# A four-layer graph network on one core: transposes moved from TensorE to DVE blocks and transfers, and three engines' order written out

## The chip, the cores and the metric

One Trainium2 chip, one of its cores. The metric is the device time of one execution in microseconds (us); the program runs on core 0 alone, in float32 throughout. The engines are called by their short names: PE (TensorE, matmuls), PEld (its weight loads), DVE (VectorE), ACT (ScalarE), POOL (GpSimd) and SP (SyncE, here only a queue that issues DMAs).

## The reference

128 graphs of 64 nodes with 256 features pass through four layers, each followed by a residual sum and a layer norm. Every layer uses the same weighted adjacency `adj` (128 x 64 x 64), which is not symmetric.

```python
# --- layer 0: five node groups (25 of the 64 nodes), two graph convolutions each
x = _layernorm(x + _L0_gnn_ref(x, adj, W1, b1, W2, b2, fusion_w))
# --- layer 1
A = adj + eye;  dinv = A.sum(-1) ** -0.5
x = _layernorm(x + (dinv[:, :, None] * A * dinv[:, None, :]) @ (x @ W) + b)
# --- layer 2
An = adj / (adj.sum(2, keepdims=True) + 1e-9);  c = h = x @ W.T
out = w[0] * c
for k in (1, 2, 3):
    c = An @ c;  out = out + w[k] * c
x = _layernorm(x + leaky_relu(out + b, 0.2))
# --- layer 3: five steps of a gated recurrent cell, A = (adj != 0)
h = x
for l in range(5):
    agg = A.T @ (h @ weight[l])
    r = sigmoid(agg @ Wir + h @ Whr + b);  z = sigmoid(agg @ Wiz + h @ Whz + b)
    n = tanh(agg @ Win + bin + r * (h @ Whn + bhn))
    h = (1 - z) * n + z * h
x = _layernorm(x + h * mask)
```

## The kernel before

**Tiling.** The 128 graphs are cut into 16 chunks of 8 graphs. Two graphs lie side by side on the 128 partitions (64 nodes each), and a chunk holds four such pairs of graphs: a tile of node states is 128 x 4 x 256. An adjacency of two graphs is a 128 x 128 block-diagonal square. Layer 3 keeps its state the other way round, features on the partitions (`hT`, `hn`: 128 x 2 x 512), so that the gate products stream 256 columns; products 1 to 7 of each gate are a scheme with seven products (factored weights `V`, `WHH`; differences `Ta`, `Th` from `sums`, L746, on POOL) in place of eight.

**Stages.** The first 300 us are layer 0 over all graphs, in 16 units; layers 1 and 2 of chunks 0 and 1 are fitted into its last units (`early`, two instances of `mid`). Then come the folded weights, and then the loop, which is layer 3 for all chunks. Chunks run in pairs: step s works on chunk `rows[s % 2]`, so the two chunks of a pair take turns, five layers each, ten steps to a pair. Steps of a pair are called 0 to 9 here; step 8 is layer 5 of the even chunk, step 9 that of the odd one. While a pair is in the loop, `mid` (L220) does layers 1 and 2 of the next pair in parts, each part ending at a `yield`; `next(filler)` in `step` runs one part. In a step, PE multiplies for x; the other chunk w is finished at the start (`new(3)`), and gets its messages near the end.

**`mid`.** Part 1, on DVE: the block-diagonal `Ab` is the loaded adjacency times a 0/1 `pair` mask (L227), then `A01`, row sums, `dg`, `An`. Part 2: four PE transposes of `Ab` (L259), evicted by DVE into `poly` (L262) and `AT1` (L264, L265). Part 3: a product `pp`, its eviction (L273) and layer 1's gather (L212). Part 4: `xt` plus bias (L277) and the last polynomial. Parts 5 and 6: layer 1's products, norm. Parts 7 to 9: layer 2 and its norm.

**The change of pairs.** After its fifth layer a chunk's `hn` is turned back into node order: `flip` (L881) turns 32 x 32 blocks on DVE (L888), writes them to DRAM (L893) and reads them back permuted (four reads, L897) into `h`. `output` (L991) adds `h` to `xt` with eight DVE instructions (L998) and takes the norm's statistics; `close` (L1001) scales on ACT and stores. The new chunk's first `hT` comes from layer 2's result by eight PE transposes (L810) and two ACT copies (L817), in `state_of_layer2` (L813).

**What sets the order.** PE's order is written out by hand for the whole program (`manual_schedule`), ACT's for the loop. DVE, POOL and the DMA queue SP are ordered by a planner with costs and due times of its own; each engine then runs its list in order and waits at semaphores. `issue_after` and `high_priority` are hints to that planner. A tile with `bufs=n` has n buffers that take turns; a new use waits for the last reader of the old one. PSUM is two pools of 5 (`pg`) and 3 (`pt`) banks.

Of the kernel before, what the change touches and what calls it, by code (L numbers as in the profile page):

```python
# [24 lines left out]
CB = 8  # L25
# [43 lines left out]
def gnn_stack(  # L69
# [21 lines left out]
    c_pair: bass.AP,  # L91
# [34 lines left out]
    def norm_stats(y, by="v", n=NP, r=128):  # L126

        by = (by * n)[:n]
        st = small.tile([128, NP, 6], F32, name="st")
        mv = small.tile([128, NP, 2], F32, name="mv")  # L130
        for p in range(n):
            nc.vector.bn_stats(st[:r, p, :], y[:r, p, :])  # L132
            nc.vector.bn_aggr(mv[:r, p, :], st[:r, p, :])
        ve = small.tile([128, NP], F32, name="ve")
        nc.vector.tensor_scalar(ve[:r, :n], mv[:r, :n, 1], EPS_LN, None, op0=ALU.add)  # L135
        rs = small.tile([128, NP], F32, name="rs")
        nc.gpsimd.tensor_tensor(rs[:r, :n], ve[:r, :n], mhalf[:r, :n], ALU.pow)  # L137
        nb = None
        if "a" in by:
            nb = small.tile([128, NP], F32, name="nb")  # L140
            nc.vector.scalar_tensor_tensor(nb[:r, :n], mv[:r, :n, 0], -1.0, rs[:r, :n], op0=ALU.mult, op1=ALU.mult)
        return mv, rs, nb
# [11 lines left out]
    def layernorm(y, by="v", n=NP, r=128):  # L154
        norm_apply(y, *norm_stats(y, by, n, r), by, n, r)
# [10 lines left out]
    av = adj.rearrange("(c p two) n m -> c (two n) p m", p=NP, two=2)  # L166
# [20 lines left out]
    def load_adj(c):  # L187
        a64 = keep.tile([128, NP, N], F32, name="a64", bufs=2)
        nc.sync.dma_start(a64, av[c])
        adjs[c] = a64  # L190
# [27 lines left out]
    state = {}  # L218

    def mid(c, first=False):  # L220

        a64 = adjs.pop(c)


        Ab = keep.tile([128, NP, 128], F32, name="Ab", bufs=1)
        with tc.issue_after(evictions[-1].ins):
            nc.vector.tensor_mul(  # L227
                Ab.rearrange("p q (b m) -> p q b m", b=2),
                a64[:, :, None, :].to_broadcast([128, NP, 2, N]),
                pair[:, None, :, :].to_broadcast([128, NP, 2, N]),  # L230
            )
        A01 = keep.tile([128, NP, 128], F32, name="A01", bufs=4)
        nc.vector.tensor_scalar(A01, Ab, 0.0, None, op0=ALU.not_equal)
        rsum = small.tile([128, NP], F32, name="rsum")
        with tc.issue_after(evictions[-1].ins):
            nc.vector.tensor_reduce(rsum, a64, AX.X, ALU.add)
# [5 lines left out]
        dinv1 = inv_sqrt(rdeg, NP, 128, "d1")  # L242
# [13 lines left out]
        AT1 = keep.tile([128, NP, 128], F32, name="AT1", bufs=1)  # L256
        p = psum("pT1").rearrange("p (q n) -> p q n", q=NP)
        for q in range(NP):
            nc.tensor.transpose(p[:, q, :], Ab[:, q, :], ident)  # L259

        with tc.high_priority():
            nc.vector.scalar_tensor_tensor(poly, p, cw[:, 3:4], poly, op0=ALU.mult, op1=ALU.add)  # L262

        nc.vector.tensor_add(AT1, p, ident[:, None, :].to_broadcast([128, NP, 128]))  # L264
        nc.vector.tensor_mul(AT1, AT1, dinv1[:, :, None].to_broadcast([128, NP, 128]))  # L265
# [34 lines left out]
        norm_apply(xt, *norm)  # L300
# [21 lines left out]
        norm_apply(xt, *norm)  # L322
# [14 lines left out]
    with ExitStack() as c0:  # L337
# [101 lines left out]
        def hidden(i):  # L439
            u = UNITS[i]  # L440
            ag0 = AG.pop(i)
            hg = keep.tile([128, 4, 512], F32, tag="NI", name="hg", bufs=2)
            for e in range(4):
                p = psum0("ph")[:, : u.cols]
                for k in range(2):
                    nc.tensor.matmul(  # L446
                        p, W1[:, u.g, k, e * 128 : (e + 1) * 128], ag0[:, k, : u.cols], start=k == 0, stop=k == 1
                    )
                relus.append(
                    nc.scalar.activation(hg[:, e, : u.cols], p, AF.Relu, bias=b1[:, u.g * 4 + e : u.g * 4 + e + 1])  # L450
                )
            HG[i] = hg
# [97 lines left out]
        zero = keep.tile([128, 4, 512], F32, tag="NI", name="zero", bufs=2)[:, 0, :]  # L550
# [50 lines left out]
        for i in range(-2, NU + 1):  # L601
# [60 lines left out]
            elif i == 1:  # L662
                with tc.issue_after(powers[-1].ins):
                    pair = const_later(c_pair, [128, 2, N], "pair")
# [29 lines left out]
            elif i == g0:  # L694
                for c in (0, 1):
                    load_adj(c)
            elif i == g0 + 1:
                for c in (0, 1):
                    load_x(c)
        for _ in early:  # L700
            pass
# [98 lines left out]
    class Chunk:  # L800
# [19 lines left out]

        def messages(self):
            src = halves(self.xt)
            if self.l:
                h = self.h
                src = lambda q, k: h[:, q, 2 * k : 2 * k + 2, :]
            self.agg = gather(src, self.A01, "agg", work, "agg", 2)
            self.ta = sums(self.agg, "a")
# [20 lines left out]
        def n(self, i):  # L848
            if i == 1:
                self.NI = keep.tile([128, 2, 2, NP * 128], F32, tag="NI", name="NI", bufs=2)  # L850
                self.gn = Gates(
                    self.NI, [[(V[self.l], 2, self.agg, self.ta)], [(WHH, 2, self.hT, self.th)]], "n"
                )
            self.gn.product(i)

        def new(self, i):
# [3 lines left out]
            if i == 2:  # L860
                self.hn = work.tile([128, 2, NP * 128], F32, tag="hT", name="hn", bufs=3)
# [19 lines left out]
        def flip(self, half):  # L881
# [3 lines left out]
            if not half:  # L885
                self.h = work.tile([128, NP, NP, 64], F32, name="h", bufs=1)
            t = work.tile([128, NP, 2, 2, 32], F32, name="flip", bufs=2)
# [103 lines left out]
        def output(self):  # L991
# [7 lines left out]
            self.norm = norm_stats(self.xt, "a")  # L999
# [31 lines left out]
    before = ended = None  # L1031
    filler = iter(())

    def step(s):
        nonlocal before, ended, filler
        x, w = rows[s % 2], before
        nxt = None
        x.rz(1)
        if w:
            w.new(3)  # L1040
        x.rz(2)
        x.rz(5)
        next(filler, None)
# [4 lines left out]
        next(filler, None)  # L1048
        x.rz(7)
        x.new(2)  # L1050
        x.n(6)
        x.sigmoid(7)
        if w and w.l == L - 1 and w.c + 2 < NCH:
            nxt = Chunk(w.c + 2)
            nxt.state_of_layer2(1)
        x.n(5)
        if nxt:
            nxt.state_of_layer2(0)
# [4 lines left out]
        if ended:  # L1063
            ended.close()
            ended = None
# [4 lines left out]
        elif w:  # L1070
            w.output()
            ended = w
            if nxt:
                nxt.messages()
                rows[(s + 1) % 2] = nxt
        x.sigmoid(3)
# [6 lines left out]
    for s in range(NCH * L - 1):  # L1083
        u, t = s // (2 * L) * 2, s % (2 * L)
        if t == 0:
            for _ in filler:
                pass
            if u + 2 < NCH:
                for c in (u + 2, u + 3):
                    load_adj(c)  # L1090
                    load_x(c)
                filler = both(mid(u + 2), mid(u + 3))
        with tc.manual_schedule(engines={mybir.EngineType.Activation}):
# [10 lines left out]
    x.NI = keep.tile([128, 2, 2, NP * 128], F32, tag="NI", name="NI", bufs=2)  # L1104
# [5 lines left out]
    norm = norm_stats(w.xt)  # L1110
# [10 lines left out]
def _constants():  # L1121
    ident = np.eye(128, dtype=np.float32)
    b128 = np.arange(128) // N
    pair = np.repeat((b128[:, None] == np.arange(2)[None]).astype(np.float32), N, axis=1).reshape(128, 2, N)
# [11 lines left out]
    return {"ident": ident, "pair": pair, "block0": block, "eye0": eye}  # L1136
# [44 lines left out]
```

## Time and profile before

| what | number |
|---|---|
| median of 3 runs | 2156.74 us (2156.57 to 2156.82) |
| the profiled execution, its own time | 2156.53 us |
| its span, first to last instruction | 2154.8 us, 31383 instructions |
| granted PE clock, mean | 0.999 |
| DMA | 133.05 MB, 386411 packets, mean 62 GB/s |
| a pair's ten steps | 231.1 us (windows from 564.6 on) |

In what follows, a line of a group reads: line of the kernel, engine, operation, output <- input (buffer numbers left out), shapes and count | busy us in total, mean ns of one | idle time of the engine just before, and what ended it. PSUM tiles named `pT1`, `pT3`, `pT4` all appear as `pT`. A line of the timeline reads: start in us, length in us, engine, line, operation, count of merged ones, and in brackets how long the engine had been idle and who released it. A matmul's length includes the pipeline, so the pitch of matmuls is read from starts. A float32 matmul call appears as two instructions, a transpose as one.

### The profile page before, as it was taken

How to read it: one execution, taken by the hardware profiler on the slowest of the kernel's cores; microseconds unless marked ns; L12 is line 12 of the kernel's file. 1: busy time of each engine (PE TensorE's matmuls, PEld its weight loads, DVE VectorE, ACT ScalarE, POOL GpSimd, SP SyncE). 2: the span in 40 equal slices, each digit the busy share in tenths (PEclk: the TensorE clock that was granted, in tenths of full speed). 3: DMA queues.
4: the chain of work that ended last, by engine and by line, in shares of the span. 5: the costliest groups of instructions: out<-in, count | busy, mean ns of one | idle time of the engine just before them, and what ended most of it. 6: DMA issues, size and time to landing. Idle time of an engine off the chain costs nothing.

```text
span 2154.8 us, 31383 instructions
## 1 busy us (share of the span) xinstructions
PE 2112.3 (98%) x10914; PEld 1844.1 (86%) x10914; DVE 1558.6 (72%) x3821; ACT 991.4 (46%) x2034; POOL 592.8 (28%) x634
## 2 busy tenths in 40 slices
PE   9999999999999999999999999999999999999997
PEld 6777888988888888988888889888898889888886
DVE  3345667776878778867887697868877787768666
ACT  3343344444454444444545445444445454454444
POOL 3311131322322323322322232223322232322222
PEclk9999999999999999999999999999999999999999
DMA  6632110221221222121321222122221221122121
GB/s 168 180 126 63 54 38 23 51 51 46 68 69 40 55 52 74 48 54 48 85 50 40 59 62 62 40 59 62 66 53 40 56 73 40 48 51 72 47 59 40
DMA packets 386411, 133.05 MB, mean 62 GB/s; under 512 B 353102, under 2 KB 381260, under 8 KB 386252
## 3 DMA queue, kind: packets, MB, share of 16 engines
q1 hardware_dynamic: 381380, 125.79, 22.6%
q0 software_dynamic: 2160, 4.83, 0.9%
q8 instruction: 87, 1.43, 0.3%
q10 hardware_dynamic: 2712, 0.42, 0.1%
q14 instruction: 72, 0.59, 0.1%
HBM read 73.30 MB, written 57.67 MB: 61 GB/s over the span
## 4 chain that ended last, share of the span: by engine, by line
PE 84%; DVE 13%; DMA 1%; issue 1%; POOL 1%; ACT 0%; SPq 0%; ACTq 0%; DVEq 0%; POOLq 0%
PE parz L769 22%; PE pdrz L769 11%; PE pan L769 11%; PE pa L212 8%; PE pbrz L769 5%; PE pdn L769 5%; PE ps L462 5%; PE ph L446 4%; PE pbn L769 3%; PE pd L311 3%; DVE xt L998 2%; PE pd L290 2%; PE pa L430 1%; DVE st L132 1%; PE po L484 1%
## 5 line engine op out<-in xcount | busy, mean ns | idle before, releaser
L786 ACT COPY c<-parz 128x512 f32<-128x512 f32 x240 | 140.1, 584 | 407.6 <-PE parz L769 407.6
L769 PE MATMUL parz<-Th,WHH 128*128 128x256 f32 x960 | 286.6, 380 | 11.5 <-ACT c L786 11.5
L769 PE MATMUL parz<-Ta,V 128*128 128x256 f32 x960 | 285.5, 379 | 0.0
L910 ACT ACTIVATE NI<-NI,bih 128x256 f32<-128x256 f32 x316 | 159.4, 507 | 186.7 <-DVE NI L905 183.7
L844 ACT ACTIVATE RZ<-RZ,brz 128x256 f32<-128x256 f32 x474 | 215.0, 503 | 51.2 <-DVE RZ L788 41.9
L749 POOL TENSOR_TENSOR Ta<-agg 128x512 f32<-128x512 f32 x80 | 102.3, 1279 | 490.6 <-ACT agg L214 490.1
L769 PEld LDWEIGHTS parz<-Th,WHH 128*128 128x128 f32 x960 | 177.8, 190 | 35.6 <-ACT c L786 13.9
L769 PEld LDWEIGHTS parz<-Ta,V 128*128 128x128 f32 x960 | 182.4, 190 | 24.8
L137 POOL TENSOR_TENSOR rs<-ve,mhalf 128x4 f32<-128x4 f32 (+2 forms) x65 | 68.2, 1049 | 484.7 <-DVE ve L135 432.7
L214 ACT COPY agg<-pa 128x512 f32<-128x512 f32 x160 | 93.0, 586 | 151.4 <-PE pa L212 151.4
L792 DVE TENSOR_TENSOR NI<-pbn,c 128x512 f32<-128x512 f32 x79 | 54.3, 688 | 139.0 <-ACT c L786 139.0
L749 POOL TENSOR_TENSOR Th<-hn 128x512 f32<-128x512 f32 x64 | 81.5, 1274 | 244.3 <-DVE hn L913 244.3
L904 DVE SCALAR_TENSOR_TENSOR NI<-NI,bhh,RZ 128x256 f32<-128x256 f32 x237 | 142.0, 599 | 4.9
L769 PE MATMUL pan<-Ta,V 128*128 128x256 f32 x474 | 141.4, 380 | 0.8 <-ACT c L786 0.7
L769 PE MATMUL pan<-Th,WHH 128*128 128x256 f32 x474 | 141.0, 379 | 0.0
L786 ACT COPY c<-pan 128x512 f32<-128x512 f32 x237 | 137.2, 579 | 7.8 <-PE pan L769 4.4
L912 DVE TENSOR_TENSOR RZ<-RZ 128x256 f32<-128x256 f32 x316 | 128.7, 407 | 1.9
L212 PEld LDWEIGHTS pa<-A,h 128*128 128x128 f32 x1024 | 124.4, 192 | 4.3 <-issue 1.0
L913 DVE TENSOR_TENSOR hn<-RZ,NI 128x256 f32<-128x256 f32 x316 | 125.7, 415 | 3.2
L788 DVE TENSOR_TENSOR NI<-pdn,c 128x512 f32<-128x512 f32 x79 | 54.4, 689 | 99.3 <-ACT c L786 99.3
L212 PE MATMUL pa<-A,h 128*128 128x128 f32 x1024 | 124.8, 275 | 0.6 <-issue 0.6
L888 DVE STREAM_TRANSPOSE flip<-hn 128x512 f32<-128x512 f32 x156 | 108.9, 698 | 0.0
(229 smaller groups left out, 4887.6 us busy)
## 6 DMA issues: line engine op xcount, KB each, us to landing
hb<-flip SPq DMA_DIRECT2D x156, 256.0 KB
h<-hb SPq DMA_DIRECT2D x624, 64.0 KB
out_dram<-xt SPq DMA_DIRECT2D x30, 256.0 KB
W<-in_w_dram SPq DMA_DIRECT2D x10, 512.0 KB
xt<-xb SPq DMA_DIRECT2D x32, 156.0 KB
xo<-in_x_dram SPq DMA_DIRECT2D x9, 512.0 KB
xb<-xo SPq DMA_DIRECT2D x9, 512.0 KB
xt<-xa SPq DMA_DIRECT2D x32, 100.0 KB
```

The costliest lines, as they stand in the source:

```text
L212: nc.tensor.matmul(p[:, q * 128 : (q + 1) * 128], src(q, k), m[:, q, :], start=True, stop=True)
L214: nc.scalar.copy(a[:, k, :], p)
L462: nc.tensor.matmul(p[: u.rows[t], t - v, :], hg[:, e, u.off[t] : u.off[t] + u.rows[t]], W2[:, u.g, e, :], start=e == 0, stop=e == 3,)
L749: nc.gpsimd.tensor_sub(t[:, 0:2, :], a[:, :, H:], a[:, 0, :].rearrange("p (s n) -> p s n", s=2))
L769: nc.tensor.matmul(bank[:, g, :], w[:, q, i - 1, :], rhs, start=i in (1, 2, 5) and g == 0 and m == 0, stop=m == len(side) - 1, skip_group_ ...
L786: nc.scalar.copy(c, self.a)
L844: nc.scalar.activation(v, self.g.a[:, q, :] if i == 4 else v, AF.Sigmoid, bias=brz[:, 2 * q + j : 2 * q + j + 1])
L888: nc.vector.transpose(t.rearrange("p r q j f -> p q j r f"), self.hn[:, :, half * H : (half + 1) * H].rearrange("p j (q r f) -> p q j r f" ...
L904: nc.vector.scalar_tensor_tensor(n[:, j, f], h, bhh[:, 4 + j : 5 + j], r[:, j, f], op0=ALU.add, op1=ALU.mult)
L910: nc.scalar.activation(n, n, AF.Tanh, bias=bih[:, 4 + j : 5 + j])
L912: e.tensor_mul(d, d, z)
L913: e.tensor_add(self.hn[:, j, f], d, n)
```

## The change

- Layer 2's result is turned into `hT` by `state_by_transfer`: a DVE block transpose of each half, one write to DRAM and four reads per half. It is called a step earlier than the PE version was, at layer 5 of x. The first two chunks keep `state_of_layer2`. `sums` of the new `hT` is called at the next step's start.
- The adjacency comes in twice: into the diagonal blocks of `Ab`, which is now one buffer zeroed once, and in 32 x 32 blocks into `aB`, which DVE turns into the diagonal blocks of `AT1`, zeroed once too. The mask product, the constant `pair` and the PE transposes in `mid` are gone. Loads of adjacency and states are placed at steps 3 and 8.
- The filler runs at two places of a step, at one in step 0. `norm_stats` is split: the pow and `nb` are in `norm_root`. `output`'s norm is finished a step later, and `close` is a step later and at the step's start. New messages come before `output`.
- ACT, SP and POOL all follow the program's order over the whole loop.
- Buffers: `NI` one instead of two, with `hn` of the last layer written into it; `h` two instead of one; `hg` of layer 0 takes turns between two pools.

```diff
-    def norm_stats(y, by="v", n=NP, r=128):
+    def norm_stats(y, n=NP, r=128):
...
+        return mv, ve
+
+    def norm_root(mv, ve, by="v", n=NP, r=128):
+        by = (by * n)[:n]
         rs = small.tile([128, NP], F32, name="rs")
         nc.gpsimd.tensor_tensor(rs[:r, :n], ve[:r, :n], mhalf[:r, :n], ALU.pow)
...
     def load_adj(c):
-        a64 = keep.tile([128, NP, N], F32, name="a64", bufs=2)
-        nc.sync.dma_start(a64, av[c])
-        adjs[c] = a64
+        aB = keep.tile([128, NP, N], F32, name="aB", bufs=1)
+        ac = adj[c * CB : (c + 1) * CB].rearrange("(p two) n m -> two n p m", two=2)
+        for two in range(2):
+            b = slice(two * N, (two + 1) * N)
+            nc.sync.dma_start(Ab[b, :, b], ac[two])
+        for two in range(2):
+            for r in range(2):
+                o = two * N + 32 * r
+                for v in range(2):
+                    nc.sync.dma_start(
+                        aB[o : o + 32, :, 32 * v : 32 * v + 32], ac[two, 32 * v : 32 * v + 32, :, 32 * r : 32 * r + 32]
+                    )
+        adjs[c] = aB
...
+    Ab = keep.tile([128, NP, 128], F32, name="Ab")
+    AT1 = keep.tile([128, NP, 128], F32, name="AT1")
     def mid(c, first=False):
...
         with tc.issue_after(evictions[-1].ins):
-            nc.vector.tensor_mul(
-                Ab.rearrange("p q (b m) -> p q b m", b=2),
-                a64[:, :, None, :].to_broadcast([128, NP, 2, N]),
-                pair[:, None, :, :].to_broadcast([128, NP, 2, N]),
-            )
-        A01 = keep.tile([128, NP, 128], F32, name="A01", bufs=4)
+            for two in range(2):
+                b = slice(two * N, (two + 1) * N)
+                nc.vector.transpose(AT1[b, :, b], aB[b])
...
-            nc.vector.tensor_reduce(rsum, a64, AX.X, ALU.add)
+            nc.vector.tensor_reduce(rsum, Ab, AX.X, ALU.add)
...
-        p = psum("pT1").rearrange("p (q n) -> p q n", q=NP)
-        for q in range(NP):
-            nc.tensor.transpose(p[:, q, :], Ab[:, q, :], ident)
-
+        dinv1 = inv_sqrt(rdeg, NP, 128, "d1")
         with tc.high_priority():
-            nc.vector.scalar_tensor_tensor(poly, p, cw[:, 3:4], poly, op0=ALU.mult, op1=ALU.add)
-
-        nc.vector.tensor_add(AT1, p, ident[:, None, :].to_broadcast([128, NP, 128]))
-        nc.vector.tensor_mul(AT1, AT1, dinv1[:, :, None].to_broadcast([128, NP, 128]))
+            nc.vector.scalar_tensor_tensor(poly, AT1, cw[:, 3:4], poly, op0=ALU.mult, op1=ALU.add)
+
+        nc.vector.tensor_add(AT1, AT1, ident[:, None, :].to_broadcast([128, NP, 128]))
+        for two in range(2):
+            b = slice(two * N, (two + 1) * N)
+            nc.vector.tensor_mul(AT1[b, :, b], AT1[b, :, b], dinv1[b, :, None].to_broadcast([N, NP, N]))
...
+                    for t in (Ab, AT1):
+                        nc.gpsimd.memset(t, 0.0)
...
+        def state_by_transfer(self):
+            self.hT = work.tile([128, 2, NP * 128], F32, tag="hT", name="hT", bufs=3)
+            for j in range(2):
+                t = work.tile([128, NP, NP, 32], F32, tag="flip2", name="flip2", bufs=2)
+                nc.vector.transpose(
+                    t.rearrange("p a q n -> p q a n"),
+                    self.xt[:, :, j * 128 : (j + 1) * 128].rearrange("p q (a i) -> p q a i", a=NP),
+                )
+                hb = dram.tile([NP, NP, NP, 32, 32], F32, name="hb2", bufs=2)
+                nc.sync.dma_start(
+                    hb.rearrange("a q r i n -> (r i) (a q) n"), t.rearrange("p a q n -> p (a q) n")
+                )
+                for a in range(NP):
+                    nc.sync.dma_start(
+                        self.hT[32 * a : 32 * (a + 1), j, :].rearrange("p (g n) -> p g n", n=32),
+                        hb[a].rearrange("q r i n -> i (q r) n"),
+                    )
...
     def step(s):
-        nxt = None
+        nxt = coming.pop() if coming else None
         x.rz(1)
         if w:
             w.new(3)
+        if closing:
+            closing.close()
+        closing, ended = ended, None
+        if nxt:
+            nxt.th = sums(nxt.hT, "h")
         x.rz(2)
         x.rz(5)
-        next(filler, None)
+        if s % (2 * L):
+            next(filler, None)
...
-        next(filler, None)
         x.rz(7)
         x.new(2)
+        c = s // (2 * L) * 2 + {3: 3, 8: 4}.get(s % (2 * L), NCH)
+        if c < NCH:
+            load_adj(c)
+            load_x(c)
         x.n(6)
         x.sigmoid(7)
-        if w and w.l == L - 1 and w.c + 2 < NCH:
-            nxt = Chunk(w.c + 2)
-            nxt.state_of_layer2(1)
+        if closing:
+            closing.norm = norm_root(*closing.norm, "a")
+        if x.l == L - 1 and x.c + 2 < NCH:
+            coming.append(Chunk(x.c + 2))
+            coming[-1].state_by_transfer()
         x.n(5)
-        if nxt:
-            nxt.state_of_layer2(0)
...
-        if ended:
-            ended.close()
-            ended = None
         x.rz(3)
...
         elif w:
-            w.output()
-            ended = w
             if nxt:
                 nxt.messages()
                 rows[(s + 1) % 2] = nxt
+            w.output()
+            ended = w
...
-        with tc.manual_schedule(engines={mybir.EngineType.Activation}):
+    ordered = {mybir.EngineType.Activation, mybir.EngineType.SP, mybir.EngineType.Pool}
+    with tc.manual_schedule(engines=ordered):
+        for s in range(NCH * L - 1):
...
             step(s)
```

## The prediction

> **What bounds the kernel now.** I read the page's first part, then PE's waits, then single stretches of the loop (windows, timeline, groups by shape), last the DMA part. The page (busy time by engine; shares of the chain):
>
> ```profile
> PE 2112.3 (98%) x10914; PEld 1844.1 (86%) x10914; DVE 1558.6 (72%) x3821; ACT 991.4 (46%) x2034; POOL 592.8 (28%) x634
> PE 84%; DVE 13%; DMA 1%; issue 1%; POOL 1%; ACT 0%; SPq 0%; ACTq 0%; DVEq 0%; POOLq 0%
> ```
>
> PE is never out of work for long: 2154.8 - 2112.3 = 42.5 us in all. A gain must come from fewer PE instructions or from those 42.5 us. PE's waits (releaser, total, times, longest) show where these lie:
>
> ```profile
> PE parz L769 <- ACT c L786: 11.5, 8, 2.0
> PE pa L212 <- DVE poly L273: 8.3, 6, 1.4
> PE pdrz L769 <- DVE RZ L788: 5.6, 6, 1.0
> ```
>
> Six or eight times each, in a loop that changes to a new pair of chunks seven times: 25.4 us, 3.6 at a change. The windows of one change, steps 9, 0 and 1 of the ten (length, then busy PE, PEld, DVE, ACT, POOL, clock, DMA share, GB/s):
>
> ```profile
> 761.40:782.26 20.86, 20.86 (x110) 18.57 (x109) 13.32 (x29) 10.59 (x23) 5.72 (x7) 1.00 0.21 51
> 782.26:809.64 27.38, 24.45 (x138) 21.66 (x137) 26.20 (x68) 14.14 (x30) 7.74 (x9) 1.00 0.24 63
> 809.64:835.21 25.57, 24.53 (x125) 21.60 (x124) 23.66 (x60) 10.57 (x24) 7.22 (x9) 1.00 0.29 77
> ```
>
> In step 0 DVE is busy 26.20 of 27.38 us and PE is the one that waits, 2.93 us. Everywhere else PE rules. The granted clock is 1.00 in all three, so it enters no term.
>
> **The PE transposes that go.** Starts of four in a row and of what follows (start, length, what):
>
> ```profile
> 1792.75 0.60 PE L259 MATMUL pT<-ident,Ab 128*128 128x128 f32 x4
> 1793.19 0.60 PE L769 MATMUL parz<-Th,WHH 128*128 128x256 f32 x2
> ...
> 1951.90 0.60 PE L810 MATMUL pT<-ident,xt 128*128 128x128 f32 x4
> 1952.34 0.60 PE L769 MATMUL parz<-Th,WHH 128*128 128x256 f32 x2
> ```
>
> Four take 0.44 us of PE's row, 0.11 each; the groups' 272 ns is a length in the pipeline, not a pitch. Counts and the work beside them:
>
> ```profile
> L810 PE MATMUL pT<-ident,xt 128*128 128x128 f32 x128 | 19.2, 273 | 0.9 <-DVE V L737 0.9
> L259 PE MATMUL pT<-ident,Ab 128*128 128x128 f32 x64 | 9.6, 272 | 0.0
> L817 ACT COPY hT<-pT 128x512 f32<-128x512 f32 x32 | 17.2, 582 | 1.0 <-PE pT L810 1.0
> L888 DVE STREAM_TRANSPOSE flip<-hn 128x512 f32<-128x512 f32 x156 | 108.9, 698 | 0.0
> L227 DVE TENSOR_TENSOR Ab<-a,pair 128x512 f32<-128x512 f32 x16 | 10.9, 679 | 4.9 <-PE pT L259 4.9
> ```
>
> All 64 of the adjacency go. Of the 128 of layer 2's result, the first two chunks keep 16 (the first pair still calls `state_of_layer2`), so 112 go. 176 x 0.109 = **19.2 us** off PE, where PE is full. Ends: the groups' busy time (0.15 each) would give 26.4; if DVE or a transfer holds the same spots, 0. I take 19.2, since pitch is what PE's row is made of. The 28 copies L817 (16.3 us of ACT, 46% busy) are worth nothing by themselves.
>
> [...]
>
> **What DVE gains.** Per chunk: two flips of xt, 128x512 like L888, +1.4 us; the product L227 goes, -0.68; two half-height block transposes of 256 elements, each between half of L888 and all of it, +0.7 to +1.4; the row sum over 512 instead of 256 elements (L236 takes 402 ns), 0 to +0.4; the product with dinv1 in two halves of 256 elements (L905 takes 0.42 us) instead of one of 0.68, +0.16. Together 1.6 to 2.7; I take 1.9. Over 16 chunks some 30 us, DVE from 72 to 74%: in most steps hidden under PE (step 9: DVE 13.32 of 20.86), on the path only in step 0. If that cover failed everywhere, all 30 would show.
>
> **The change of pairs, the term that I had to choose.** Now step 0 holds a chunk's `output` (eight L998), its norm, and three parts of `mid`. After, only the first part of `mid` runs in step 0; parts 2 and 3 fall into step 1, and the pow and `nb` of the closing norm move a step on (DVE waits 0.50 us for that pow at 791.14 now). Step 0 loses from DVE L262, L264, L265, L273 and L227, 0.6 to 0.7 us of pitch each, 3.1, and L277 of part 4, 1.1; it gains about 1.0 of block transposes and row sum. Contention falls too. The same instruction, alone and beside POOL:
>
> ```profile
> 785.54 0.34 DVE L998 SCALAR_TENSOR_TENSOR xt<-h,mask,xt 128x128 f32<-128x128 f32 x1
> ...
> 808.88 3.21 DVE L998 SCALAR_TENSOR_TENSOR xt<-h,mask,xt 128x128 f32<-128x128 f32 x4
> ```
>
> 0.34 against 0.80 us: the second lies under POOL's Ta (808.77 on), another three under Th at 802. The change computes Th early in the step, so three or four of the eight are freed: -1.4. DVE's step 0 comes to 26.2 - 3.1 - 1.1 + 1.0 - 1.4 = 21.6 us. PE's comes to 19.9: 42 matmul calls of 0.43 and one gather of 1.78, since transposes and `mid`'s products leave it. So DVE still has 1.7 too much there; in step 9 it has the second flips and `mid`'s last norm on top (13.3 + 1.3 + 1.3 = 15.9 of 19.9, which fits). The excess is paid by PE only where a product waits for its bank; step 1 has slack for the rest. Ends of the stall: 0, or 3.6 as now, or, if all the excess shows and step 9 adds 2, 5. I take 2.0 at a change, the excess and a little for step 9, since the last change stalls too (2.0 of the 11.5, at 1956) though no `mid` runs there: 7 x 2.0 = 14 instead of 25.4.
>
> **Edits that I cost at nothing.** Adjacency: two plain and eight block transfers per chunk for one, some 10 x 0.4 us of SP's queue (L189 takes 0.40), one to two steps before they are read; if late, `mid`'s first part waits, and PE one step later. NI in one buffer: its next writer (L792) already follows the last flip on DVE (794.41, then 795.67), so order covers it; without it, a stall of that 0.7 us. hn in NI for the last layer likewise. ACT's `close` one step later: ACT is at 46%. POOL's order: `Th` of the new chunk waits at a step's start for its transfers, and behind it stand `mid`'s and the closing pows; covered while the transfers end in time (below). Two memsets and one layer-0 buffer shared differently: once. Layer 0's stages keep their PE order less 8 transposes, counted above.
>
> **The transfers.** Flip, write, read, from the chain (start, length), and the queue's line on the page:
>
> ```profile
> 564.05 2.74 DMA hb<-flip
> 567.65 1.85 DMA h<-hb
> ...
> q1 hardware_dynamic: 381380, 125.79, 22.6%
> ```
>
> That queue's packets take 22.6% x 16 x 2154.8 / 381380 = 20.4 ns. A chunk's new path has two writes of 2048 and eight reads of 512 packets of 128 B, 8192 packets; at 20.4 ns on 16 engines 10.4 us, 14 chunks 146 us: DMA from 23 to about 30%. As a chain: twice (write issue 0.4 to 0.75, landing 2.7 to 5, four issues of 0.45 to 0.9) and 1.85, that is 12 to 21 us; I take 16. It starts some 13 us into the step and is read by `Th` at the next step's start and by PE a step after that, 25 us or more later, so PE does not meet it.
>
> [...]
>
> **The sum**, against the profiled execution: 2156.53 us (span 2154.8 and 1.7 around it; the median is 2156.74). 2156.5 - 19.2 - 25.4 + 14 = **2126**.
>
> **Rivals.** (1) The stalls go entirely, as DVE's order puts part one of `mid` into step 1: 2156.5 - 19.2 - 25.4 = 2112. For it: what is moved has a step of slack. Against: the last change. (2) The stalls stay at 3.6 or reach 5: 2137 to 2147. For it: DVE is still over PE in step 0. (3) Slower: SP's one queue. In steps 9 and 0 the two writes of the new chunk wait for DVE, each read for its write, and the flips of the old chunk's last layer stand behind them, now in a fixed order. Their h feeds L998, and DVE is in order: when h lands later than DVE's place for L998, everything behind it waits, and soon PE. The old chunk's h lands now about 18 us into step 0 (800.6). I expect 20 or 21. The price is the lateness past that place, at each of 14 chunks; slower than before needs 44.6 us less 14 already counted, 30.6 / 14 = 2.2 us more per chunk; chains of 21 us, 5 more than I take, would give 14 x 5 = 70 us uncovered, at half cover 35: 2161. Against it: DMA is busy 0.24 there.
>
> **How the numbers follow.** Forecast 0.47 (own range 2116 to 2133); rival 1, 0.20 (2107 to 2115); rival 2, 0.18 (2134 to 2154, of which 0.02 is within 0.2%, about what a measurement of this kernel can tell from no change); rival 3, 0.15 (0.01 within 0.2%, 0.14 above). Faster 0.47 + 0.20 + 0.16 = 0.83, same 0.03, slower 0.14. The range 2110 to 2150 leaves out rival 3, some of rival 1 below 2110, and the top of rival 2.
>
> **What would show it.** PE's count falls by 176 to 10738, L259 is gone, 16 of L810's pT<-ident,xt remain; plain steps still take 19.9 us; PE's waits on c, poly and RZ total about 14. Wrong: new waits of DVE on h<-hb or of POOL's Th above 5 us with PE idle behind them (rival 3), or L998 still at 0.8 us.

## The result and the profile after

The changed kernel takes **2204.93 us** (median of 4, 2203.65 to 2207.08) against 2156.78 before: ratio 1.0224, 95% interval 1.0207 to 1.0242. The profiled execution is 2206.19 us (span 2204.1, granted clock 0.990). The forecast was 2126 us, faster.

The page's lines that answer to those of before: busy time by engine, and the shares of the chain that ended last.

```profile
PE 2117.5 (96%) x10738; PEld 1832.8 (83%) x10738; DVE 1603.6 (73%) x3881; ACT 974.3 (44%) x2006; POOL 605.0 (27%) x635
PE 64%; DVE 18%; DMA 5%; SPq 4%; ACT 4%; issue 2%; POOL 2%; ACTq 0%; DVEq 0%; POOLq 0%
```

The 176 transposes are gone (10914 to 10738), and yet PE is busy 5.2 us longer, and idle 86.6 us (2204.1 - 2117.5) instead of 42.5. PE's waits:

```profile
PE parz L777 <- ACT c L794: 26.5, 17, 2.6
PE pan L777 <- ACT c L794: 18.9, 23, 2.0
PE pT L419 <- DVE A L411: 15.3, 2, 14.4
PE pdrz L777 <- POOL Ta L757: 7.6, 6, 1.5
```

The third is new and in layer 0; the others are in the loop. The starts of the steps (their first product for the gates) divide the loss: the loop begins 17.1 us later (344.6 instead of 327.5), its first seven pairs take 1639.0 instead of 1609.6 us (29.4 more), and the rest 2.9 more. That is 49.4, and the span grew by 49.3. The mean of pairs 2 to 6 grows from 231.1 to 235.9 us. The windows of the steps 9, 0 and 1 that correspond to those shown of before, each taken from 1.5 us ahead of the step's first product (783.79, 806.27 and 827.26) to as far ahead of the next step's (length, busy PE, PEld, DVE, ACT, POOL, clock, DMA share, GB/s):

```profile
782.29:804.77 22.48, 20.45 (x102) 17.56 (x101) 20.57 (x46) 9.40 (x21) 7.32 (x7) 1.00 0.46 90
804.77:825.76 20.99, 20.45 (x102) 17.58 (x101) 17.55 (x43) 9.51 (x21) 2.95 (x3) 1.00 0.29 47
825.76:855.00 29.24, 24.81 (x126) 20.96 (x125) 24.04 (x56) 12.95 (x28) 10.52 (x11) 0.94 0.37 94
```

Step 0 is relieved, as forecast (27.38 to 20.99). Step 1 takes 29.24 us; with the same parts of `mid` at the same places it needs 22.7 when nothing is late (experiment 4). Step 9 takes 22.48; before it took 20.8, and without the eight transposes that left it (0.87) that would be 19.9.

**Layer 0.** The timeline of DVE:

```profile
97.19 0.15 DVE L122 SCALAR_TENSOR_TENSOR d0o<-deg,d0r 126x4 f32<-126x4 f32 x1
119.12 0.43 DVE L242 TENSOR_SCALAR A<-Ab 128x512 f32<-128x512 f32 x1 [21.78 <-DMA Ab<-in_adj_dram]
```

L242 is `A01`, `mid`'s first look at the adjacency. Before, it came behind the mask product, and that was held back by `issue_after`. Now it reads the loaded `Ab` directly, only the block transposes carry the hint, and the planner put it ahead of layer 0's own work on DVE. The load is issued at 111.9 us; DVE stands for 21.8 us, and PE behind it for 14.4; the window from 116 to 132 has a granted clock of 0.72.

**Step 1.** POOL in the same stretch, in its fixed order:

```profile
827.23 1.27 POOL L757 TENSOR_TENSOR Th<-hT 128x512 f32<-128x512 f32 x1 [18.72 <-DMA hT<-hb]
...
830.26 1.19 POOL L140 TENSOR_TENSOR rs<-ve,mhalf 128x4 f32<-128x4 f32 x1
831.42 1.29 POOL L757 TENSOR_TENSOR Ta<-agg 128x512 f32<-128x512 f32 x1
...
837.18 1.27 POOL L757 TENSOR_TENSOR Th<-hn 128x512 f32<-128x512 f32 x1 [2.80 <-DVE nb L144]
...
840.01 1.01 POOL L120 TENSOR_TENSOR d1r<-d1s,mhalf 128x4 f32<-128x4 f32 x1
```

POOL reaches Th of the new state in step 0 and stands 18.72 us for its transfers. Then a norm's pow and Ta follow without a gap, beside the gates on DVE. `mid`'s pow d1r comes only behind the Th of the other chunk's new `hn`, for which POOL waits 2.80 us on DVE. ACT, in its fixed order too, a little before:

```profile
837.14 2.07 ACT L152 ACTIVATE xt<-xt,nb,rs 128x256 f32<-128x256 f32 x4 [1.49 <-DVE nb L144]
839.12 0.71 ACT L263 ACTIVATE poly<-dg,cw 128x512 f32<-128x512 f32 x1
839.74 0.56 ACT L794 COPY c<-parz 128x512 f32<-128x512 f32 x1
```

PE's stops in this step, and how fast it runs after the second:

```profile
832.76 0.70 PE L777 MATMUL pdrz<-Ta,V 128*128 128x256 f32 x2 [1.45 <-POOL Ta L757]
...
837.18 0.59 PE L777 MATMUL pbn<-hT,WHH 128*128 128x256 f32 x2
840.35 0.70 PE L777 MATMUL parz<-Th,WHH 128*128 128x256 f32 x2 [2.58 <-ACT c L794]
...
843.28 1.22 PE L777 MATMUL pan<-Ta,V 128*128 128x256 f32 x2 [0.41 <-ACT c L794]
844.29 0.99 PE L777 MATMUL pan<-Th,WHH 128*128 128x256 f32 x2
845.12 0.60 PE L777 MATMUL pdn<-Ta,V 128*128 128x256 f32 x2
845.55 0.59 PE L777 MATMUL pdn<-Th,WHH 128*128 128x256 f32 x2
```

The first stop is POOL's order: `agg` was there at 826.3, and Ta stood behind the waiting Th. The second is ACT's order: the bank copy c stands behind `close` (L152) and `poly`, and `close` waited for nb on DVE. From about 841.7, 1.3 us after the second stop, two matmuls start 1.01 us apart instead of 0.43, until 845.1: the waits cost more than they show. The windows 840.30 to 843.30 and 843.30 to 846.00 have a granted clock of 0.73 and 0.67, so 0.27 x 3.0 + 0.33 x 2.7 = 1.7 us. Not each such stop does this: at five of the six stops of 2.6 us in this kernel's loop the clock was half for 3.4 us, from between 0.5 us before the stop's end and 1.3 us after it; at the sixth, which ends at 1075.29, it stayed at 1.00 (window 1070 to 1085). The stop's length alone does not decide. Experiment 1, whose longest wait in the loop is 2.6 us too, was granted 0.996 over its run. That leaves about three such stretches, an estimate: 0.004 x 2184.8 x 2 = 17.5 us at half the clock, less 7.3 at the end of the run as in this kernel (from 2196.8 on), is 10.2.

### The profile page after: what moved, and what is told of

Its sections match the earlier page's. It is cut to its first block, busy times and chain, and to the rows that moved or that the text cites. A ratio compares the mean times of both kernels' runs of the same rounds, so it can differ in the third digit from the quotient of the medians.

```text
span 2204.1 us, 31432 instructions
## 1 busy us (share of the span) xinstructions
PE 2117.5 (96%) x10738; PEld 1832.8 (83%) x10738; DVE 1603.6 (73%) x3881; ACT 974.3 (44%) x2006; POOL 605.0 (27%) x635
## 3 DMA queue, kind: packets, MB, share of 16 engines
q1 hardware_dynamic: 516996, 142.58, 26.6%
## 4 chain that ended last, share of the span: by engine, by line
PE 64%; DVE 18%; DMA 5%; SPq 4%; ACT 4%; issue 2%; POOL 2%; ACTq 0%; DVEq 0%; POOLq 0%
PE parz L777 16%; PE pan L777 9%; PE pdrz L777 8%; PE pa L224 7%; PE pdn L777 4%; PE pbrz L777 4%; PE ps L468 3%; PE ph L452 3%; DMA hb<-flip 3%; PE pd L296 3%; DVE NI L934 2%; PE pbn L777 2%; DVE RZ L941 2%; DVE NI L935 2%; DVE RZ L942 1%
## 5 line engine op out<-in xcount | busy, mean ns | idle before, releaser
L777 PE MATMUL parz<-Th,WHH 128*128 128x256 f32 x960 | 291.1, 385 | 26.5 <-ACT c L794 26.5
L757 POOL TENSOR_TENSOR Ta<-agg 128x512 f32<-128x512 f32 x80 | 103.0, 1288 | 642.3 <-ACT agg L226 642.3
L757 POOL TENSOR_TENSOR Th<-hn 128x512 f32<-128x512 f32 x64 | 81.4, 1272 | 319.9 <-DVE hn L943 289.0
L777 PE MATMUL pan<-Ta,V 128*128 128x256 f32 x474 | 146.4, 391 | 19.4 <-ACT c L794 18.9
L942 DVE TENSOR_TENSOR RZ<-RZ 128x256 f32<-128x256 f32 x316 | 139.1, 442 | 2.7
L934 DVE SCALAR_TENSOR_TENSOR NI<-NI,bhh,RZ 128x256 f32<-128x256 f32 x237 | 130.4, 550 | 4.1
L941 DVE TENSOR_TENSOR RZ<-hn,NI 128x256 f32<-128x256 f32 x252 | 106.2, 421 | 18.4 <-ACT NI L940 17.4
L935 DVE TENSOR_TENSOR NI<-NI 128x256 f32<-128x256 f32 x237 | 113.1, 477 | 3.2
L777 PEld LDWEIGHTS pan<-Ta,V 128*128 128x128 f32 x474 | 80.7, 192 | 38.4 <-ACT c L794 32.6
L943 DVE TENSOR_TENSOR hn<-RZ,NI 128x256 f32<-128x256 f32 x256 | 108.7, 444 | 2.3
```

The lines of the kernel that those rows point to most:

```text
L757: nc.gpsimd.tensor_sub(t[:, 0:2, :], a[:, :, H:], a[:, 0, :].rearrange("p (s n) -> p s n", s=2))
L777: nc.tensor.matmul(bank[:, g, :], w[:, q, i - 1, :], rhs, start=i in (1, 2, 5) and g == 0 and m == 0, stop=m == len(side) - 1, skip_group_ ...
L934: nc.vector.scalar_tensor_tensor(n[:, j, f], h, bhh[:, 4 + j : 5 + j], r[:, j, f], op0=ALU.add, op1=ALU.mult)
L935: nc.vector.tensor_add(n[:, j, f], i, n[:, j, f])
L941: e.tensor_sub(d, self.hT[:, j, f], n)
L942: e.tensor_mul(d, d, z)
```

## The experiments

My theory was that two things are wrong that have nothing to do with PE's work: layer 0's early read (A), and the transfers of the new state with the fixed POOL order behind them (B). All kernels start from the changed one unless said otherwise.

**1. Hold `A01` back.**

```diff
-        nc.vector.tensor_scalar(A01, Ab, 0.0, ...)
+        with tc.issue_after(evictions[-1].ins):
+            nc.vector.tensor_scalar(A01, Ab, 0.0, ...)
```

> The changed kernel, but the 0/1 adjacency A01 of mid's first part may not be put ahead of layer 0's latest eviction on DVE (as the mask product was before). Theory A (DVE sits 21.8 us behind the adjacency's transfer in layer 0 because A01 was planned there early): the 14.6 us PE stall near 116 us goes and with it the half-speed clock behind it, 2206 - 15 to 19 = 2187 to 2191, the loop unchanged. Rival (the adjacency is simply late, the next reader waits as long): 2200 or more.

2187.60 us, 1.0139 (1.0124 to 1.0154): 17.3 less. The loop starts at 327.7, and the mean of pairs 2 to 6 stays at 235.87. Shown: 17 us are this one operation's place.

**2 and 3. The fixed order.** ACT's alone fixed, as before the change; then ACT's and SP's.

```diff
-    ordered = {Activation, SP, Pool}
+    ordered = {Activation}          # and: {Activation, SP}
```

> The changed kernel with ACT alone in written order in the loop; SP and POOL are planned, as before the change. Theory B (POOL's written order puts Th of the state ahead of the pow that d1o needs and ahead of Ta, DVE blocks 3.3 us, PE stalls 1.45 + 2.6 us and then runs at half clock for a while, at each of 6 to 7 changes): 25 to 40 us gone, 2166 to 2181. Rival C (DVE simply has too much in steps 9 to 1, whatever POOL's and SP's order): within 8 us of 2206.

> The changed kernel with ACT and SP in written order, POOL planned. Theory B (POOL): as the run with ACT alone, 2166 to 2181. Rival D (SP's queue: the old chunk's flips stand behind the new chunk's transfers): only the run that also frees SP gets faster, this one stays at 2200 or more.

2312.75 us, 1.0717 (1.0701 to 1.0733), and 2230.46, 1.0340 (1.0322 to 1.0357): both worse than the change. PE's waits of the first, then of the second:

```profile
PE pbrz L777 <- DMA hT<-hb: 118.4, 7, 17.1
```

```profile
PE parz L777 <- POOL Th L758: 35.7, 7, 5.4
```

The planner puts the new state's transfers, or its Th, too late, once a pair. The planned orders are worse than the written one, so B's forecast falls. Whether another written order would be better, these two runs do not say (7 to 11 do).

**4 and 5. The new state by PE again**, in the place of `state_by_transfer`, everything else as changed; then the same with edit 1.

```diff
-            for j in range(2): ...          # flips, writes, reads
+            for k in (1, 0):
+                p = self.transpose(lambda q, k: self.xt[...], k, "pT3")
+                nc.scalar.copy(self.hT[:, k, :], p)
```

> The changed kernel, but the new chunks' hT comes from PE transposes and ACT copies at the place where the DVE blocks and transfers were (a step earlier than in the kernel before); everything else as changed. PE gets 112 x 0.11 = 12.3 us back. Theory B: Th no longer waits for transfers, so Ta's 1.45 us go (about 9), the 2.6 us of the pow stay: 2206 + 12 - 9 = 2205 to 2212. Rival D (the transfers and their queue are the loop's loss): 2206 + 12 - 30 = 2185 to 2195.

> The changed kernel with both edits that each took time off: A01 behind layer 0's latest eviction, and the new chunks' hT from PE transposes. If the two losses are apart in time and add (layer 0's stall 17, the transfers' net loss 29): 2206 - 17 - 29 = 2158 to 2163, no better than before, so that what is left of the change (7 us of adjacency transposes less on PE, order, filler) is worth nothing. Rival (they share a cause): 2170 or more.

2177.00 us, 1.0089 (1.0074 to 1.0104), and with the guard 2158.65, 1.0005 (0.9996 to 1.0015). PE does 112 transposes more and the kernel is 27.9 us faster; step 1 falls from 28.87 to 22.73 in the mean of pairs 2 to 6. It lands below both numbers on record, on the side of rival D. The two losses add: 17.3 + 27.9 = 45.2, and together 46.3. So in this schedule the transfers' path costs about 28 us more than the transposes that it replaces. Which part of the path (POOL's wait, the two flips on DVE, the queue) does it, this swap does not say. And with both edits the kernel takes as long as the one before, though PE has 64 transposes fewer: what is left of the change gives nothing here. Step 9 stays at 22.85 us with PE's transposes.

**6. The kernel before with the adjacency's part alone** (loads into `Ab` and `aB`, at steps 2 and 6; the filler stays at its places).

> The kernel before with the adjacency's part of the change alone: zeroed Ab and AT1, block transfers, DVE transposes, no pair mask, A01 behind layer 0's latest eviction; the adjacency and states of the next chunks are loaded in steps 2 and 6, filler in three places, order of SP and POOL planned as before. PE loses 64 x 0.11 = 7.0 us. Theory (DVE's 0.7 us more per chunk are hidden when the first part runs early): 2146 to 2152. Rival (step 0 is full, the stalls there grow by as much): 2155 or more.

2163.49 us, 1.0028 (1.0017 to 1.0038): 64 transposes fewer, and slower. PE's waits on c and RZ are 16.1 and 12.1 us, where before has 11.5 and 5.6: in the mean of pairs 2 to 6 step 0 goes from 27.38 to 27.07 us and step 1 from 25.57 to 26.88. The rival has the number (2155 or more), but the growth is in step 1, not in the full step 0. That DVE's added work makes it is argued, not shown; the pow of `mid` also moves to part 2, as in the change.

**7 to 11. Places.** The question became where `mid`'s parts and Th lie. With edit 1: the filler at three places of every step, with the loads in steps 2 and 6; Th of the new state behind `new(2)`; both; and three places with PE's transposes, once with Th early and once with Th late.

```diff
-        if s % (2 * L):
-            next(filler, None)
+        next(filler, None)                  # three places: every step,
...
         x.n(2)
+        next(filler, None)                  # and here
...
-        if nxt:                             # Th late: from here
-            nxt.th = sums(nxt.hT, "h")
         x.rz(2)
...
         x.new(2)
+        if nxt:                             # to here
+            nxt.th = sums(nxt.hT, "h")
-        c = ... {3: 3, 8: 4} ...
+        c = ... {2: 3, 6: 4} ...
```

> The changed kernel with A01 behind layer 0's latest eviction and the filler run at three places of every step, as before the change, so that mid of both new chunks ends in step 5 and not in step 9; loads in steps 2 and 6. The transfers of hT stay. Theory E (the odd chunk's layer 2 ends only in step 9, its flips come 7 us into step 0, hT lands at the end of step 0, and Th stands before the pow and Ta on POOL): the step-1 stall of 6 us and those of steps 4 and 9 (1.4 and 2.6) mostly go, 2188 - 7 x 8 = 2132 to 2150. Rival F (the transfers cost as much whenever they run, since flips and reads share SP): 2175 or more.

> As the kernel with filler at three places, but hT from PE transposes. Theory E: with transfers in time this is the slower of the two by the 12.3 us of PE work: 2145 to 2160. Rival F: it is the faster of the two, by 20 us or more.

> The changed kernel with A01 behind layer 0's latest eviction, and the new chunk's Th computed after new(2), in the middle of a step, instead of at its start: on POOL it then stands behind the first filler part's pow. Theory G (what the transfers cost is POOL's written order: Th waits for hT and everything behind it waits with it): the 1.4 us of Ta and part of the step-1 stall go, 2188 - 10 to 25 = 2163 to 2178. Rival F (the transfers cost by SP's queue): 2184 to 2190.

> The kernel with filler at three places (2179), with the new chunk's Th computed after new(2). The pows of mid's parts 1 and 2 then stand ahead of Th on POOL. Theory G: PE's wait of 30.8 us on AT (7 times, 5.1 at most) and the clock's loss behind it go, 2179 - 40 to 55 = 2124 to 2140. Rival F: 2170 or more.

> The fastest kernel so far (filler at three places, Th after new(2), 2136) with hT from PE transposes. By the forecast's term it is 12.2 us slower: 2146 to 2151. If the transfers cost stalls there too: 2142 or less.

| edit 1 and | new state by transfers | by PE |
|---|---|---|
| two places, Th early | 2187.60 | 2158.65 |
| two places, Th late | 2200.54, 1.0201 (1.0186 to 1.0216) | |
| three places, Th early | 2179.20, 1.0099 (1.0083 to 1.0114) | 2155.04, 0.9989 (0.9979 to 0.9998) |
| three places, Th late | **2136.45, 0.9904 (0.9889 to 0.9919)** | 2150.24, 0.9972 (0.9959 to 0.9984) |

Each move alone gives little (-8.4) or harm (+12.9); together they give -51.1. With Th early, three places give rival F its numbers twice: 2179 is over 2175, and PE's transposes are 24.2 us faster. Th late with two places (2200.54) is above what either side gave. PE's waits of the kernel with three places and Th early, with POOL's timeline, point to Th's place:

```profile
PE pa L224 <- DVE AT L272: 30.8, 7, 5.1
```

```profile
795.51 1.28 POOL L758 TENSOR_TENSOR Th<-hT 128x512 f32<-128x512 f32 x1 [6.30 <-DMA hT<-hb]
...
798.69 1.19 POOL L120 TENSOR_TENSOR d1r<-d1s,mhalf 128x4 f32<-128x4 f32 x1
```

`mid`'s pow d1r, which layer 1's gather waits for by way of L272, stands on POOL behind a Th that waits for transfers and whose products run only in the next step. With Th late the pow is first, Th waits about as long, and nobody behind it does:

```profile
782.53 1.19 POOL L120 TENSOR_TENSOR d1r<-d1s,mhalf 128x4 f32<-128x4 f32 x1
789.39 1.28 POOL L758 TENSOR_TENSOR Th<-hT 128x512 f32<-128x512 f32 x1 [5.67 <-DMA hT<-hb]
```

That kernel is 21.0 us below the kernel before as measured beside it. Its page line, and the windows of its steps 9, 0 and 1 (again from 1.5 us ahead of each):

```profile
PE 2099.0 (98%) x10738; PEld 1830.5 (86%) x10738; DVE 1569.6 (74%) x3881; ACT 976.7 (46%) x2006; POOL 596.0 (28%) x635
```

```profile
758.93:778.85 19.92, 19.92 (x102) 17.77 (x101) 14.28 (x29) 9.63 (x21) 5.66 (x6) 1.00 0.56 106
778.85:801.44 22.59, 22.59 (x126) 20.45 (x125) 20.86 (x51) 11.10 (x24) 8.55 (x8) 1.00 0.42 83
801.44:825.91 24.47, 24.47 (x126) 21.63 (x125) 21.87 (x61) 11.49 (x25) 6.37 (x7) 1.00 0.24 65
```

PE is never idle in the three. In this schedule the transfers are worth 2150.24 - 2136.45 = 13.8 us. With three places and Th early they cost 24.2, with two places 2187.60 - 2158.65 = 29.0. So with three places Th's place alone decides whether they cost or give; rival F, the transfers' cost by their queue, falls there.

**12 to 15. Around the best one.** Its pow d1r back in part 1; its adjacency as before the change; its second load in step 8 instead of 6. And the two-place kernel of edit 1 with the second load in step 9 instead of 8.

> As the last, and the pow for dinv1 in mid's first part. Theory G: it is already ahead of Th there, so within 6 us of the run without this edit. If DVE's d1o still waits behind something else, it is faster by more than that.

> The fastest kernel so far (filler at three places, Th after new(2), 2136) with the adjacency as before the change: one load, pair mask, four PE transposes in mid. If the forecast's term for the adjacency holds where nothing stalls: 7 us slower, 2141 to 2146. Rival (DVE's extra block transposes and row sums cost as much as PE saves, as in the run with the adjacency alone): 2132 to 2138.

> The fastest kernel so far with the second load in step 8 instead of step 6. Theory H: the first part then falls into steps 8 to 0 instead of 6 and 7; step 7's wait for h (1.2 to 2 us a pair) goes, but steps 9 and 0 get the work: 2130 to 2145, with step 7 at 20 us and step 0 above 22.6.

> The changed kernel with A01 behind layer 0's latest eviction and the second load of adjacency in step 9 instead of step 8, so that DVE's list can't have the next pair's first part in steps 8 and 9. Theory H (that part, pulled forward, is what makes steps 9 and 0 stall): step 9 falls from 22.8 to 20 to 21 us, 2188 - 10 to 20 = 2168 to 2178, unless step 0 or 1 takes it up again. Rival (Th and the pow alone): 2184 to 2192.

2140.42 us, 0.9928 (0.9912 to 0.9945): the pow's place matters little, 4.0 us with runs from 2136.4 to 2144.8. 2145.27, 0.9942 (0.9925 to 0.9958): the adjacency's part is worth 8.8 us, or 4.9 against the first of these runs, which has the pow in part 1 as this one has. 2143.51, 0.9935 (0.9920 to 0.9950): a later load costs 7.1 here (step 0 grows from 22.6 to 24.8 us, step 7 falls from 21.7 to 20.0). And 2176.54, 1.0088 (1.0073 to 1.0103), 11.1 less than edit 1: step 9 falls from 22.76 to 20.83, so that stall goes with the load's place: part 1 of `mid`, pulled forward by DVE's planner once its load is in. Step 1 takes up 1.0 of it (28.62 to 29.66).

**16 to 18. What is left with two places.** Th late and the pow in part 1; these with the load in step 9; these with `close` behind `new(2)` on ACT:

```diff
-        if closing:
-            closing.close()
-        closing, ended = ended, None
+        late, closing, ended = closing, ended, None
...
         x.new(2)
+        if late:
+            late.close()
```

> As the kernel with Th in the middle of the step, and the pow for dinv1 back in mid's first part, as before the change, so that in step 1 d1o no longer waits for it. Theory G: the 3.3 us for which DVE sits on d1o go too, and the half-speed clock behind that PE stall: another 7 x 3 to 6, 2135 to 2160. Rival F: no change against the run without this edit.

> The changed kernel, filler at two places as in it, with A01 behind layer 0's latest eviction, the second load in step 9, Th after new(2) and the pow of dinv1 in mid's first part. If these are the whole loss, step 1 falls from 29.7 us to 23 to 25 and the whole to 2176 - 6 x 5 = 2140 to 2152, below the kernel before. If something else holds step 1 (DVE's load, the transfers), 2165 or more.

> The kernel with two filler places and all four other repairs, and `close` on ACT moved from the step's start to behind `new(2)`, after Th of the new state. Theory K (ACT runs in order; `close` stands there for nb, which DVE computes only behind the late products of the same step, and poly and PE's bank copy c stand behind it): step 1 falls from 29.2 us to 23 to 26 us, the waits of PE's parz for c from 31.8 us to under 18, and the time from 2177 to 2140 to 2160 us. Rival L (DVE itself, which carries part 1's products, two gates and a half-height turn in a stretch where POOL runs ten products beside it, is what is late, and ACT's wait only shows it): step 1 stays at 28 us or more and the time within 8 us of 2177.

2192.17 us, 1.0165 (1.0150 to 1.0180); 2177.23, 1.0093 (1.0072 to 1.0115); 2189.02, 1.0150 (1.0133 to 1.0167). All three missed what my own theory gave. In the second, ACT's `close` waits 3.30 us for nb on DVE and the bank copy c stands behind it; the third takes that away: the waits of PE's parz for c fall from 31.8 to 12.6 us, as forecast, but those of pan rise from 12.8 to 44.7, and step 1 goes from 29.2 to 30.4. What the last one's ACT and PE wait for:

```profile
824.93 0.91 ACT L872 ACTIVATE RZ<-RZ,brz 128x256 f32<-128x256 f32 x2 [6.09 <-DVE RZ L801]
825.74 0.56 ACT L795 COPY c<-pan 128x512 f32<-128x512 f32 x1
```

```profile
826.36 0.98 PE L778 MATMUL pan<-Ta,V 128*128 128x256 f32 x2 [4.74 <-ACT c L795]
```

L801 is DVE's sum for the gates, at 824.20; DVE's timeline has no gap from 809.5 to 824.9. In that stretch it holds the end of a step's gates, and from `mid` `dg`, `An`, the first polynomial and most of `AT1`. So the theory that ACT's order is the cause falls, and the rival stands in its first number (step 1 at 28 or more), though the time went 11.8 us up, past its 8. With three places and Th late, step 1 holds none of those four. What the runs leave open: the third place moves `mid`'s parts and the loads together, and no run of two places thins out step 1's DVE alone.

## Why the prediction was wrong, step by step

**PE's work: right.** 176 transposes went, at 19.2 us. Split as 7.0 for the adjacency and 12.2 for the state, the term measures 4.9 to 8.8 and 13.8 in the kernel where nearly nothing else is late. The 0.11 us pitch was the right price, the group's 272 ns the wrong one.

**"Edits that I cost at nothing": the step that failed**, with the cover that it leaned on. Four of its items cost time.

- "POOL's order ... covered while the transfers end in time." They did not end in time: Th waited 18.72 us, and Ta and a norm's pow stood behind it. I had named what stands behind Th and priced it at nothing. The path costs 27.9 us (experiment 4). That Th's place is what makes it cost is shown with three places (from 24.2 lost to 13.8 gained). With two places it is not: Th late alone is 12.9 us worse, and how the loss divides between POOL's order and DVE's load stays open there.
- "ACT's `close` one step later: ACT is at 46%." That share says nothing of order: c waits behind `close`, and PE stops for 2.58 us. Moving `close` later in the step did not help either (experiment 18), so what delays nb on DVE is part of it.
- The loads, "one to two steps before they are read". I priced a late load and not an early one: with the second load in step 8, part 1 of `mid` runs in step 9. A step later the whole is 11.1 us faster.
- "Layer 0's stages keep their PE order": true of PE, but DVE's order is the planner's, and the edit that took away the mask product took its hint away too. That is 17 us, shown by experiment 1.

**The transfers: size right, place wrong.** I took 16 us from 12 to 21; from the first write's issue (814.25) to Th (827.23) it is 13.0. But I started it 13 us into step 9, where the program writes it. DVE gets to the odd chunk's flips 7.2 us into step 0:

```profile
812.79 0.69 DVE L155 TENSOR_SCALAR xt<-xt,mv,rs 128x256 f32<-128x256 f32 x2
813.51 1.31 DVE L834 STREAM_TRANSPOSE flip<-xt 128x512 f32<-128x512 f32 x2
```

L155 is the norm that makes what is flipped. So the step of slack, which was the whole of the cover, was not there: `hT` lands as PE's first product of step 1 reads it (827.26).

**The change of pairs: 14 us forecast, some 77 measured.** The sum's own balance gives it: 2206.2 - (2156.5 - 19.2 - 25.4) = 94.3, less 17.1 for layer 0, 77.2 for seven changes, 11 each, where I took 2.0. In the means of pairs 2 to 6, step 1 is 6.1 over its quiet length (28.87 against 22.73), step 9 3.0 (22.91 against 19.92), step 0 1.1. Step 1's excess goes with the transfers (experiment 4); step 9's stays with PE's transposes and mostly goes with the later load. I balanced DVE's busy time against PE's for step 0 alone (21.6 forecast; 18.42 from 806.27 to 827.26) and took step 1's slack as given. The work went to step 9 (19.70, I had 15.9) and to step 1, and there a busy sum under PE's, 24.04 of 29.24, did not help: the order of what DVE, POOL and ACT do first decided. "It enters no term", said of the clock, was wrong as well: seven stretches of 3.4 us at half the clock in the loop are some 12 of the 77 us.

**The rivals.** The third named the right side and the wrong place: the wait of PE's pa for h is 2.5 us in all, and nothing stood behind a late L998 (now L1028). Its 2161 was short by 44. But the sign that I gave for it, POOL's Th above 5 us with PE idle behind it, is what came. Rivals 1 and 2 fall with the main case. One item of the forecast was right and went unpaid: L998 is freed. Of its 112 instances 43 took over 0.6 us before, all under an instruction of POOL; 3 do after.

**DVE's added work: too high, and its contention too low.** I took 30 us more over the run (28, had I counted the flips at 14 chunks and not 16); DVE's busy time grew by 45.0. To split it I took the 20th percentile of each form of DVE instruction as its undisturbed length and summed what instances stretched by 30% or more take beyond that. The sum is 66 us before, 91 after and 63 in the best kernel, nearly all under an instruction of POOL (in the changed kernel 175 of 181 instances). So by this split, an estimate, 25 us are contention and 20 added work; the best kernel, with the same count of DVE instructions, gives 14 for the work. What was freed at L998 came back at the gates and the norms. DVE's last product of a gate, ns least, median and most, after and in the best kernel:

```profile
L943 DVE TENSOR_TENSOR hn<-RZ,NI x256: 384/413/1479, 358.7 to 2157.5; 128x256 f32<-128x256 f32 x128
```

```profile
L944 DVE TENSOR_TENSOR hn<-RZ,NI x256: 393/412/427, 344.9 to 2088.0; 128x256 f32<-128x256 f32 x128
```

In the changed kernel six of them take 1.48 us, of which POOL is at work for 1.40. The rows read as a wait of DVE for POOL: two L943 that start at 831.17 and 831.51 end at 832.98, 0.27 us after POOL's L757 (831.42 to 832.71), and L806, with one input in PSUM, takes its usual 0.68 us at 832.91 under POOL's next. It is so under POOL's subtractions as a whole: of the gates' DVE products and sums of 128x256 with both inputs in SBUF that start with over 0.3 us of a subtraction still to run, 99 of 100 take more than 0.53 us in the changed kernel, where each line's median is 0.41 to 0.43; of L935 with an input in PSUM (`pan`) none of 65. Under a pow of POOL on 128x4, about 1 us long, none of 22 does. Why the one holds DVE up and the other does not is not shown.

## What to carry to other kernels

When an operation moves from a full engine to a transfer, price the place before the work: find when its first instruction really starts on its engine (not where the program writes it), and what stands behind its reader in that engine's order. Moving the same 112 transposes cost 29 us with two places and 24 with three, and gave 14 with three places and one reader put behind `new(2)`. And when an operation is deleted, look at whose scheduling hint went with it.

## What the runs showed of the hardware

- At five of the six stops of 2.6 us in PE's stream in the changed kernel's loop the granted clock fell to half for 3.4 us. It also fell at the one stop of 2.3 us and at one of two stops of 2.0 us, behind which two matmuls took 0.85 us (from 1272.28 on) and not 0.43. In the loop before, as profiled, the longest stop is 2.0 us and it never fell. What makes it fall is not shown.
- POOL's subtractions held up DVE's 128x256 products and sums with both inputs in SBUF (99 of 100 over 0.53 us, against medians of 0.41 to 0.43) and not L935 with one in PSUM (0 of 65); under its pows on 128x4 none of 22 with both inputs in SBUF took longer than 0.53 us.
- The small packets were no dearer than forecast: the queue's 516996 packets took 26.6% of 16 engines' span, 18.1 ns each, where before had 20.4.
